# Edge-list graph layer: node marks as a one-hot in place of steps, slot-major marks turned by transposing DMAs, and a constant operand table

## The chip, the core and the metric

The kernel runs on one core of one Trainium2 chip. The metric is device microseconds of one execution of the whole program. The core has five instruction streams that matter here: TensorE (PE in the profile, with its weight loads shown apart as PEld), VectorE (DVE), ScalarE (ACT), GpSimd (POOL) and SyncE (SP), which only issues DMAs.

## The reference

128 graphs of 64 nodes with 128 features each; `adj` is a symmetric 0/1 matrix with ones on the diagonal, about one entry in eight set.

```python
f_i = jnp.broadcast_to(x[:, :, None, :], (B, P, P, C))      # B=128, P=64, C=128
f_j = jnp.broadcast_to(x[:, None, :, :], (B, P, P, C))
messages = _mlp(jnp.concatenate([f_i, f_j], -1), msg weights)   # relu, layernorm, relu, layernorm, linear
messages = messages * adj[..., None]
agg = jnp.sum(messages, axis=2)
out = x + _mlp(jnp.concatenate([x, agg], -1), upd weights)
```

Each `_mlp` is three products with a relu and a layernorm after the first two. A message counts only where `adj` is 1, so only the edges have to be computed.

## The kernel before, in words

**Edges as slots.** The kernel never forms the 64 x 64 pairs. Each graph gets 640 edge slots (`CAP`), five tiles of 128. Edge number k of a graph stands in slot k, node by node. Two graphs share the 128 partitions and form a *pair* (64 pairs, index p); two pairs form a *quad* (32 quads, index q; 20 tiles, 5 chunks); two quads form a *block* (16 blocks, index b; 10 chunks). A *chunk* is 4 tiles, 512 slots; there are 160, and the main loop has one *step* per chunk.

**What a step does.** In step n the kernel issues, in this order: `layer1(n - 8)`, the second message layer of an older chunk (lines 559 and 562, into the bank `z`, relu by ScalarE into `y`, line 565); `layer0(n)`, the first layer, as a product of node features with a 0/1 selection matrix `s` (line 513, into `hps`, relu into `h`, line 516); `stats0(n - 1)`, four transposes of `h` into the bank `hT` (line 522) and their layernorm statistics on VectorE (line 526); `marks(n + 2)` (line 498, into the bank `mk`) and `compare(n + 2)` (line 505), which make `s`; and `stats1(n - 8)`, statistics of `y` on VectorE (line 572). Then come the *extras* of the step: whatever a written table of `at(step, place, function)` has put there. The order on every engine is the order of this code; there is no scheduler that moves things. The banks `mk`, `hT`, `hps` and `z` exist once each.

**How `s` is made.** Per pair, `make_tp` (line 482, VectorE) writes a tile `tp`: partition i (a node of one of the two graphs), slot k, 1 where k is less than the running edge count of node i. It is a *step* along the slots. `marks` multiplies it with a per-block table `qs` whose columns hold differences of neighbouring nodes, so that the product becomes, per slot, the source node's one-hot in 64 rows and a position to be compared with in the other 64. The table `qs` is built per block: `place` (lines 394 to 399, GpSimd), `marks_table` (lines 384 to 387, GpSimd: copies constants and zeroes), `steps` (line 429, a product with a difference matrix `dq` on TensorE) and `steps_out` (lines 436 and 437, two ScalarE copies out of the bank `ma`).

**How messages are summed per node.** `reduce` (line 656) multiplies `y` of each tile with weights `w` (slots on the partitions, 64 nodes along the row). For `w` the marks are needed with slots on the partitions: `node_marks` (line 625) multiplies each 128 x 128 piece of `tp` with a constant matrix `pick`, five products per pair into banks `ma`; `node_marks_out` (line 632) copies them out with ScalarE into `oh`; `weights` (line 641, GpSimd; VectorE in the last quad) multiplies `oh` with the inverse standard deviations `m_q`. In a cycle of five steps the pair with even p has its `node_marks` in the step that also holds `reduce` (40 PE instructions of line 656) and `rows` (lines 457 and 459), the odd one in the step after it; `weights` follow two steps after each, `reduce` three steps after the first `weights`.

**Other extras.** `rank`, `count`, `degrees` (running counts per block), `turn_x` (line 443), `rows_hi` and `rows_lo` (lines 466, 473: the node features split in two parts `abh`, `abl`), the update MLP of an older block (lines 701, 715, 725, 751), statistics arithmetic on GpSimd (lines 254 to 272), `root1_of` (line 278, ScalarE, tile `m_sq`) and `inverse_of` (line 283, VectorE, tile `m_q`). SyncE issues the loads of `adj` (`an`) and `x` (`xn`) 20 to 25 steps ahead, and the stores of `uo` (line 754), which wait for `finish` (line 751).

Of the kernel before, what the change touches and what calls it, by code (L numbers as in the profile page):

```python
# [9 lines left out]
F32 = mybir.dt.float32  # L10
# [13 lines left out]
def tile_gnn(  # L24
# [11 lines left out]
):  # L36

# [66 lines left out]
    def load_first(b, q0, q1):  # L104
# [50 lines left out]
    nc.vector.memset(cmpt[0:N, 0:3 * CAP // 2], 1.0)  # L155
    slot = const.tile([P, CAP], F16, name="slot")
    nc.gpsimd.iota(slot, pattern=[[1, CAP]], base=0, channel_multiplier=0,
                   allow_small_or_imprecise_dtypes=True)

    dq = const.tile([P, P], F32, name="dq")  # L160
    nc.gpsimd.affine_select(out=dq, in_=ident, pattern=[[-1, P]], compare_op=ALU.not_equal,
                            fill=-1.0, base=-1, channel_multiplier=1)

    pick32 = const.tile([P, P], F32, name="pick32")
    nc.gpsimd.affine_select(out=pick32, in_=ident, pattern=[[-1, P]], compare_op=ALU.not_equal,
                            fill=-1.0, base=1, channel_multiplier=1)

    nc.gpsimd.memset(pick32[0:N, N:N + 1], 0.0)
    pick = const.tile([P, 2, N], F16, name="pick")
    nc.gpsimd.tensor_copy(pick.rearrange("p g m -> p (g m)"), pick32)  # L170
# [123 lines left out]
    def edge_path(es):  # L294
        blkp = es.enter_context(tc.tile_pool(name="blk", bufs=3))
        adp = es.enter_context(tc.tile_pool(name="adp", bufs=2))
        qsp = es.enter_context(tc.tile_pool(name="qsp", bufs=2))
# [41 lines left out]
        TP, S, H, ST0, V0, SD, SH, Y, ST1, Q, OH, WT, YS, MK = ({} for _ in range(14))  # L339
# [42 lines left out]
        def marks_table(b):  # L382
            qs = qsp.tile([P, PB, 2, P], F16, name="qs")
            nc.gpsimd.tensor_copy(qs[:, :, :, 0:N],
                                  pick.unsqueeze(1).to_broadcast([P, PB, 2, N]))
            nc.gpsimd.memset(qs[N:P, :, 0, N:P], 0.0)
            nc.gpsimd.memset(qs[0:N, :, 1, N:P], 0.0)
            blocks[b]["qs"] = qs

        def place(b):  # L390

            blk = blocks[b]
            before = adp.tile([P, PB], F32, name="before")
            nc.gpsimd.tensor_tensor(before, cumall[:, b * PB:(b + 1) * PB], blk["deg"],
                                    op=ALU.subtract)
# [3 lines left out]
            nc.gpsimd.tensor_tensor(pos, pos, blk["an"], op=ALU.mult)  # L399
            blk["pos"] = pos  # L400

# [67 lines left out]
        def rows_lo(b, half):  # L469
# [5 lines left out]
                op=ALU.subtract)  # L475
            blk["ab", half] = (lo, hi)


        def make_tp(p):

            tp = tpp.tile([P, CAP], F16, name="tp")
# [635 lines left out]
```

## Time and profile before

| | us |
|---|---|
| median of 3 runs | 645.67 (641.34 to 647.46) |
| profiled execution, whole | 640.71 |
| its span, first to last instruction | 639.0 |
| TensorE busy | 615.1 |
| VectorE busy | 497.6 |
| GpSimd busy | 368.4 |
| ScalarE busy | 358.6 |
| mean granted TensorE clock | 0.993 of full |

How to read it: the rows of the profile name an instruction by its line in the kernel, its engine, its operation and its tiles (out<-in), with the count, the busy time and the mean duration. Matmuls are pipelined: the duration of one (275 ns for most) is longer than the distance from one to the next, so for TensorE the start times of the timeline are the measure. A float32 product shows as two MATMUL rows, so counts of line 562 and its like are twice those of the code. The profiled execution lies 1.7 us above its span, and 5.0 us under the median of the runs.

### The profile page before, as it was taken

To read this page: it belongs to the slowest core of one execution; us is meant where nothing else is said; L and a number is where in the kernel's file an instruction comes from. 1 tells how busy PE (TensorE), PEld (TensorE's weight loads), DVE (VectorE), ACT (ScalarE), POOL (GpSimd) and SP (SyncE) were. 2 spreads that over 40 slices of the span, in tenths; PEclk is the share of its full clock that TensorE was granted. 3 is DMA by queue.
4 is the path that set the end of the run, shared out by engine and by line. 5 is a ranking of instruction groups with operands and counts; after the bars stand their busy time and mean duration, and the time that the engine had idled before them with its cause. 6 is when DMAs were issued, how large, how long until landed. Compare 5 with 4: busy or idle time off the path is not lost.

```text
span 639.0 us, 15850 instructions
## 1 busy us (share of the span) xinstructions
PE 615.1 (96%) x5875; PEld 567.0 (89%) x5875; DVE 497.6 (78%) x1894; ACT 358.6 (56%) x811; POOL 368.4 (58%) x943
## 2 busy tenths in 40 slices
PE   7899999999999999999999999999999999998875
PEld 6688899999999999999999999999999999997764
DVE  6787687878878787887878788787878877785574
ACT  3556556655656565565656556565655656563532
POOL 6742463847657384765738476573837657363653
PEclk8999999999999999999999999999999999999998
DMA  5100000010010101001010100101010000000001
GB/s 119 40 21 6 2 10 2 2 43 3 2 42 2 42 3 42 2 7 37 2 43 2 43 3 11 32 2 44 2 34 1 17 4 2 17 1 18 2 18 35
DMA packets 27916, 12.06 MB, mean 19 GB/s; under 512 B 10422, under 2 KB 27836, under 8 KB 27836
## 3 DMA queue, kind: packets, MB, share of 16 engines
q1 hardware_dynamic: 27548, 10.89, 6.4%
q8 instruction: 47, 0.77, 0.5%
q14 instruction: 33, 0.27, 0.1%
q10 hardware_dynamic: 288, 0.13, 0.1%
HBM read 6.82 MB, written 4.19 MB: 17 GB/s over the span
## 4 chain that ended last, share of the span: by engine, by line


## 5 line engine op out<-in xcount | busy, mean ns | idle before, releaser
L526 DVE BATCH_NORM_STATS2 st<-hT 128x6 f32<-128x128 f32 x640 | 141.1, 282 | 65.2 <-PE hT L522 62.6
L562 PEld LDWEIGHTS z<-w1c,h 128*128 128x128 f32 x1280 | 168.4, 192 | 7.1
L562 PE MATMUL z<-w1c,h 128*128 128x128 f32 x1280 | 168.8, 275 | 0.0
L641 POOL TENSOR_TENSOR w<-oh,m_q 128x320 f32<-128x320 f16 x124 | 86.9, 722 | 127.4 <-PE hT L522 110.9
L572 DVE BATCH_NORM_STATS2 st<-y 128x6 f32<-128x128 f32 x640 | 137.6, 276 | 6.0 <-ACT y L565 6.0
L565 ACT ACTIVATE y<-z 128x512 f32<-128x512 f32 x160 | 95.6, 597 | 81.4 <-PE z L562 79.5
L516 ACT ACTIVATE h<-hps,b0c 128x512 f32<-128x512 f32 x160 | 109.2, 682 | 6.1 <-PE hps L513 6.0
L505 DVE TENSOR_TENSOR s<-mk,cmpt 128x512 fp32r<-128x512 f32 x160 | 107.4, 672 | 0.4 <-PE mk L498 0.4
L522 PE MATMUL hT<-ident,h 128*128 128x128 f32 x640 | 97.0, 274 | 0.0
L513 PE MATMUL hps<-s,abl 128*128 128x512 f32 (+3 forms) x256 | 91.7, 370 | 0.0
L522 PEld LDWEIGHTS hT<-ident,h 128*128 128x128 f32 x640 | 76.2, 141 | 9.7
L559 PE MATMUL z<-b1t,sdT 80*128 80x512 f32 x160 | 78.8, 493 | 0.9 <-ACT y L565 0.9
L513 PE MATMUL hps<-s,abh 128*128 128x512 f32 (+3 forms) x256 | 78.1, 323 | 0.0
L656 PE MATMUL ys<-y,w 128*64 128x128 f32 x1280 | 76.9, 275 | 0.0
L656 PEld LDWEIGHTS ys<-y,w 128*64 128x64 f32 x1280 | 69.2, 137 | 3.4
L498 PE MATMUL mk<-tp,qs 128*128 128x512 f16 (+3 forms) x256 | 61.2, 300 | 1.8 <-DVE s L505 1.7
L473 DVE TENSOR_TENSOR abl<-mu,abh 128x512 fp32r<-128x512 f32 x32 | 22.1, 690 | 49.6 <-ACT abh L466 49.5
L632 ACT CAST oh<-ma 128x384 f16<-128x384 f32 (+1 forms) x128 | 48.6, 433 | 4.7 <-PE ma L625 1.8
L513 PEld LDWEIGHTS hps<-s,abl 128*128 128x128 f32 x256 | 49.2, 192 | 0.6 <-ACT h L516 0.3
L466 ACT CAST abh<-mu 128x512 fp32r<-128x512 f32 x32 | 18.7, 585 | 54.8 <-PE mu L459 54.8
L513 PEld LDWEIGHTS hps<-s,abh 128*128 128x128 f32 x256 | 49.1, 192 | 0.0
L559 PEld LDWEIGHTS z<-b1t,sdT 80*128 80x128 f32 x160 | 30.3, 190 | 8.9 <-issue 3.1
(235 smaller groups left out, 1036.8 us busy)
## 6 DMA issues: line engine op xcount, KB each, us to landing
xn<-in_x_dram SPq DMA_DIRECT2D x15, 256.0 KB, 3.2
out_dram<-uo SPq DMA_DIRECT2D x15, 256.0 KB, 2.2
an<-in_adj_dram SPq DMA_DIRECT2D x16, 128.0 KB, 2.9
xn<-in_x_dram SPq DMA_DIRECT2D x2, 128.0 KB
out_dram<-uo SPq DMA_DIRECT2D x2, 128.0 KB, 2.1
w<-in_L_gnn_msg_w_dram SPq DMA_DIRECT2D x2, 64.0 KB, 2.9
u<-in_L_gnn_upd_w_dram SPq DMA_DIRECT2D x2, 64.0 KB, 2.0
w0a<-in_L_gnn_msg_w_dram ACTq DMA_DIRECT2D x1, 64.0 KB, 2.1
```

The source lines that it names most:

```text
L498: nc.tensor.matmul(MK[n][:, c:c + w], lhsT=blocks[g // (2 * PB)]["qs"][:, g // 2 % PB, g % 2, :], rhs=TP[g // 2][:, e:e + w], start=True, ...
L505: nc.vector.tensor_tensor(S[n], MK.pop(n), cmpt[:, o:o + CH * P], op=ALU.is_equal)
L513: nc.tensor.matmul(ps[:, c:c + w], lhsT=ab[:, g % 4, :], rhs=s[:, c:c + w], start=(k == 0), stop=(k == 1))
L516: nc.scalar.activation(H[n], ps, AF.Relu, bias=b0c)
L522: nc.tensor.transpose(ps[:, t, :], H[n][:, t * P:(t + 1) * P], ident)
L526: nc.vector.bn_stats(ST0[q][:, CH * c + t, :], ps[:, t, :])
L559: nc.tensor.matmul(ps, lhsT=SD[q], rhs=W["b1t"][:, CH * c:CH * c + CH, :], start=True, stop=False, skip_group_check=True)
L562: nc.tensor.matmul(ps[:, t, :], lhsT=h[:, t * P:(t + 1) * P], rhs=W["w1c"], start=False, stop=True, skip_group_check=True)
L565: nc.scalar.activation(Y[n], ps, AF.Relu)
L572: nc.vector.bn_stats(ST1[q][:, CH * c + t, :], Y[n][:, t, :])
L641: (nc.vector if p // 2 == NQ - 1 else nc.gpsimd).tensor_tensor(w[:, :, g, :], OH[p][:, :, g, :], Q[q][:, k:k + TG].unsqueeze(2).to_broadca ...
L656: nc.tensor.matmul(YS[b][g * N:(g + 1) * N, k, :], lhsT=w[:, t, g, :], rhs=y, start=(t == 0), stop=(t == TG - 1))
```

## The change

Three things are changed together.

1. `tp` becomes a one-hot: 1 in the slots that belong to node i. ScalarE first writes a distance `d` = |mid - (2k + 1)| (`distance`, new), where `mid` is the sum of the running counts before and after the node; VectorE then compares `d` with the node's degree (`make_tp`, same shape as before). With a one-hot, the table needs no differences: `steps` (TensorE), `steps_out` (ScalarE) and `dq` go.
2. The slot-major marks `oh` are the transpose of the one-hot, so `node_marks` becomes one transposing DMA per pair, issued by SyncE, SBUF to SBUF, 128 x 640 float16. It is issued four steps earlier than the products were (two in the last quad), so six steps ahead of `weights`, whose place stays. `pick`, the five products and `node_marks_out` go. `oh` gets four buffers.
3. The table is now `qsall`, two constant halves used by blocks in turn: the identity part and the zeros are written once at the start, and `place_out` (GpSimd, two instructions on 64 partitions) writes only the positions. `marks_table` goes. `place_out` and `odd_marks` stand one step later than `place`.

```diff
+    qsall = const.tile([P, 2, PB, 2, P], F16, name="qsall")
+    for k in range(2):
+        nc.vector.memset(qsall[:, k], 0.0)
+        nc.gpsimd.tensor_copy(qsall[:, k, :, :, 0:N], ident.rearrange("p (g m) -> p g m", g=2)
+                              .unsqueeze(1).to_broadcast([P, PB, 2, N]))
...
-        def marks_table(b):
-            qs = qsp.tile([P, PB, 2, P], F16, name="qs")
-            nc.gpsimd.tensor_copy(qs[:, :, :, 0:N],
-                                  pick.unsqueeze(1).to_broadcast([P, PB, 2, N]))
-            nc.gpsimd.memset(qs[N:P, :, 0, N:P], 0.0)
-            nc.gpsimd.memset(qs[0:N, :, 1, N:P], 0.0)
...
+            blk["mid"] = adp.tile([P, PB], F32, name="mid")
+            nc.gpsimd.tensor_tensor(blk["mid"], cum, before, op=ALU.add)
...
-            nc.gpsimd.tensor_tensor(pos, pos, blk["an"], op=ALU.mult)
+        def place_out(b):
+            for g in range(2):
+                s = slice(g * N, (g + 1) * N)
+                nc.gpsimd.tensor_tensor(qsall[s, b % 2, :, g, N:P], pos[s], blk["an"][s],
+                                        op=ALU.mult)
...
-        def steps(b):
-            nc.tensor.matmul(blk["ps"][:, 0:PB * N], lhsT=dq,
-                             rhs=blk.pop("pos").rearrange("p q j -> p (q j)"), start=True,
-                             stop=True)
-        def steps_out(b):
-            nc.scalar.copy(blk["qs"][0:N, :, 0, N:P], psv[0:N])
-            nc.scalar.copy(blk["qs"][N:P, :, 1, N:P], psv[N:P])
...
+        def distance(p):
+            D[p] = tpp.tile([P, CAP], F16, name="d", bufs=3)
+            nc.scalar.activation(D[p], slot, AF.Abs, bias=blocks[b]["mid"][:, q:q + 1], scale=-1.0)
         def make_tp(p):
-            nc.vector.tensor_scalar(tp, slot, cumall[:, p:p + 1], None, op0=ALU.is_lt)
+            nc.vector.tensor_scalar(tp, D.pop(p), blocks[b]["deg"][:, q:q + 1], None,
+                                    op0=ALU.is_lt)
...
         def node_marks(p):
-            for t in range(TG):
-                nc.tensor.matmul(ps[:, k * P:(k + 1) * P], lhsT=TP[p][:, t * P:(t + 1) * P],
-                                 rhs=pick.rearrange("p g m -> p (g m)"), start=True, stop=True)
-        def node_marks_out(p):
-            for ps, t, n in zip(OH[p], (0, 3), (3, TG - 3)):
-                nc.scalar.copy(o[:, t:t + n].rearrange("p t g m -> p (t g m)"), ps[:, 0:n * P])
+            OH[p] = wp.tile([P, TG, P], F16, name="oh", bufs=4)
+            nc.sync.dma_start(OH[p], TP.pop(p), transpose=True)
...
-                at(o - 8, "e", marks_table, b)
-                at(o - 8, "e", odd_marks, b)
+                at(o - 7, "e", place_out, b)
+                at(o - 7, "e", odd_marks, b)
-                at(o - 4, "x", steps, b)
-                at(o - 3, "a", steps_out, b)
...
+                at(n - 5 if n >= 5 else 0, "a", distance, p)
                 at(n - 4, "m", make_tp, p)
-            at(m, "x", node_marks, p)
-            at(m + 1, "a", node_marks_out, p)
+            at(w - 4, "a", node_marks, p)
```

Where the rows stand, at the three places that matter. TensorE, in the step after `reduce` (the odd pair of a quad); before, `tp` is the weight operand of five products with `pick`, between the marks and the next step's `z`:

```order
L522 MATMUL hT<-ident,h 128x128 x4
L498 LDWEIGHTS qs
L498 MATMUL mk<-tp,qs 128x128
L498 LDWEIGHTS qs
L498 MATMUL mk<-tp,qs 128x384
L625 LDWEIGHTS tp
L625 MATMUL ma<-pick,tp 128x128
```

and, after four more such pairs of rows, line 559 of the next step. Of the change, the same place (line numbers are those of the changed file, 5 to 19 lower):

```order
L517 MATMUL hT<-ident,h 128x128 x4
L493 LDWEIGHTS qsall
L493 MATMUL mk<-tp,qsall 128x128
L493 LDWEIGHTS qsall
L493 MATMUL mk<-tp,qsall 128x384
L554 MATMUL z<-b1t,sdT 128x512
L557 MATMUL z<-w1c,h 128x128 x4
```

The five products are gone and the next step's `z` follows the marks at once: the step holds nothing beside its regular work.

SyncE, one block of the steady state. Before, it issues one store and two loads:

```order
L754 DMA out_dram<-uo 128x4x128
L355 DMA xn<-in_x_dram 128x4x128
L347 DMA an<-in_adj_dram 128x4x64
L754 DMA out_dram<-uo 128x4x128
L355 DMA xn<-in_x_dram 128x4x128
```

Of the change, with four transposes between the same DMAs:

```order
L736 DMA out_dram<-uo 128x4x128
L615 DMA_TRANSPOSE oh<-tp 128x5x128
L350 DMA xn<-in_x_dram 128x4x128
L615 DMA_TRANSPOSE oh<-tp 128x5x128 x2
L342 DMA an<-in_adj_dram 128x4x64
L615 DMA_TRANSPOSE oh<-tp 128x5x128
L736 DMA out_dram<-uo 128x4x128
```

Each transpose now stands behind a store or a load on one queue, and one of the four stands right behind the store that waits for `finish`.

GpSimd, from the step of `place` to the next `weights`. Before (`m_v`, `m_d`, `m_s`: statistics of a quad, which end in `m_sq` and `m_q`; `a`: `odd_marks`):

```order
L397 TENSOR_TENSOR pos<-rk,before 128x256
L399 TENSOR_TENSOR pos<-pos,an 128x256
L384 COPY qs<-pick 128x8x64
L386 MEMSET qs 64x4x64
L387 MEMSET qs 64x4x64
L417 TENSOR_TENSOR a_3252<-an 128x256
L418 TENSOR_TENSOR a_3252<-a_3252,an 128x256
L270 TENSOR_SCALAR m_v<-m_2801 128x20
L254 TENSOR_TENSOR m_d<-st_2975 128x20
```

Of the change:

```order
L384 TENSOR_TENSOR mid<-cumall,before 128x4
L386 TENSOR_TENSOR pos<-rk,before 128x256
L266 TENSOR_SCALAR m_v<-m_2699 128x20
L250 TENSOR_TENSOR m_d<-st_2871 128x20
L251 TENSOR_TENSOR m_s<-st_2871 128x20
L252 TENSOR_TENSOR m_d<-m_d 128x20
L253 TENSOR_SCALAR m_d<-m_d 128x20
L254 TENSOR_TENSOR m_3201<-m_d,m_s 128x20
L268 TENSOR_TENSOR m_v<-m_v,m_3201 128x20
L395 TENSOR_TENSOR qsall<-pos,an 64x4x64 x2
L418 TENSOR_TENSOR a_3210<-an 128x256
```

The statistics now come before the table and `odd_marks`, not behind them.

More of the change, by code (lines that the diff above doesn't have):

```diff
@@ L859, in edge_path @@
         turn_x_out(0, 0, 2)
+        degrees(0)
         place_first()
[L861 to L862 removed]
+        distance(0)
+        place_pair(0)
+        make_tp(0)
         rows(0, 0)
         rows_hi(0, 0)
[L866 to L874 removed]
+        distance(1)
+        place_pair(1)
+        make_tp(1)
         marks(0)
```

71 lines of the change are left out of this document (21 added, 50 removed).

## Prediction, on record before the result

> **What bounds the kernel now.** I read the page's busy times first, then its 40 slices, then stretches of the span, then TensorE's own starts.
>
> ```profile
> PE 615.1 (96%) x5875; PEld 567.0 (89%) x5875; DVE 497.6 (78%) x1894; ACT 358.6 (56%) x811; POOL 368.4 (58%) x943
> PE   7899999999999999999999999999999999998875
> 200.00:270.00 70.00, 70.00 (x695) 65.74 (x695) 57.67 (x223) 40.63 (x91) 41.16 (x106) 1.00 0.08 20
> 580.00:600.00 20.00, 16.14 (x156) 14.66 (x156) 12.28 (x57) 7.95 (x19) 8.90 (x20) 1.00 0.05 14
> ```
>
> A stretch reads: length, busy PE, PEld, DVE, ACT, POOL, granted clock, DMA share, GB/s. In 200 to 270 us TensorE is busy for all 70 us at full clock, VectorE for 58. The slices say the same from about 45 to 580 us. Only the start and the last 60 us have gaps. The page's chain that ended last is empty, so the waits have to say what stops TensorE; its two longest are small, with three and four cases in the whole run:
>
> ```profile
> PE ma L701 <- DVE uy L247: 4.2, 3, 2.6
> PE ma L546 <- POOL sh L541: 4.0, 4, 1.5
> ```
>
> So work taken off TensorE between 45 and 580 us shortens the program by what it occupies there, as long as nothing else comes late. What it occupies is not its busy time, since matmuls overlap. It is read from starts (start, duration, operation, count):
>
> ```profile
> 301.35 0.58 PE L559 MATMUL z<-b1t,sdT 80*128 80x512 f32 x1
> ...
> 317.44 0.60 PE L429 MATMUL ma<-pos,dq 128*128 128x256 f32 x2
> 317.88 0.27 PE L546 MATMUL ma<-ident,sh 128*80 128x128 f32 x1
> ...
> 328.04 1.05 PE L562 MATMUL z<-w1c,h 128*128 128x128 f32 x8
> 330.05 0.44 PE L625 MATMUL ma<-pick,tp 128*128 128x128 f16 x5
> 330.30 0.48 PE L559 MATMUL z<-b1t,sdT 80*128 80x512 f32 x1
> 330.62 1.05 PE L562 MATMUL z<-w1c,h 128*128 128x128 f32 x8
> ...
> 336.72 1.05 PE L562 MATMUL z<-w1c,h 128*128 128x128 f32 x8
> ...
> 338.55 0.58 PE L559 MATMUL z<-b1t,sdT 80*128 80x512 f32 x1
> 338.97 1.05 PE L562 MATMUL z<-w1c,h 128*128 128x128 f32 x8
> ...
> 341.06 0.44 PE L625 MATMUL ma<-pick,tp 128*128 128x128 f16 x5
> 341.43 2.40 PE L656 MATMUL ys<-y,w 128*64 128x128 f32 x40
> ```
>
> From one step's line 562 to the next is 2.25 us in a step without extras (336.72 to 338.97) and 2.58 in the step whose only extra is line 625 (328.04 to 330.62). The odd pair's five products cost 0.33 us. The even pair's stand in front of line 656 and cost 341.43 - 341.06 = 0.37. Line 429 costs 317.88 - 317.44 = 0.44 per block.
>
> **TensorE's part of the sum.** A quad loses 0.33 + 0.37 = 0.70 us. Of 32 quads I count 29: the last six groups of line 625 lie after 583 us, where TensorE has gaps and waits decide. 29 x 0.70 = 20.3. Line 429 runs for blocks 1 to 15: 15 x 0.44 = 6.6. Together **26.9 us**. The most it could be, with every pair and the even price, is 64 x 0.37 + 6.6 = 30.3.
>
> **The other engines, by rows.**
>
> ```profile
> L632 ACT CAST oh<-ma 128x384 f16<-128x384 f32 (+1 forms) x128 | 48.6, 433 | 4.7 <-PE ma L625 1.8
> L437 ACT CAST qs<-ma 64x256 f16<-64x256 f32 x15 | 5.5, 367 | 0.2
> L449 ACT COPY xnT<-ma 128x512 f32<-128x512 f32 (+1 forms) x16 | 9.1, 572 | 16.6 <-PE ma L443 16.6
> L482 DVE TENSOR_SCALAR tp<-slot,cumall 128x640 f16<-128x640 f16 x64 | 24.4, 383 | 0.0
> L399 POOL TENSOR_TENSOR pos<-pos,an 128x256 f32<-128x256 f32 x15 | 11.2, 744 | 1.2
> L384 POOL COPY qs<-pick 128x512 f16<-128x512 f16 x16 | 9.8, 614 | 0.1
> L387 POOL MEMSET qs<- 64x256 f16 x16 | 4.9, 308 | 0.9
> L394 POOL TENSOR_TENSOR before<-cumall,deg 128x4 f32<-128x4 f32 x15 | 3.0, 201 | 3.9 <-ACT deg L380 3.9
> ```
>
> ScalarE loses 48.6 us of line 632 and two rows like line 437 (11.0), and gains 64 distances of 640 columns. No row shows one. From the copy of 512 columns, 572 x 640 / 512 = 0.72 us, 46 in all; not under 0.57 (fewer columns), and at the rate of line 632, which carries 320 columns in 0.433, 0.87, 55 in all. ScalarE ends 4 to 23 us lighter. The copies of the even pair leave a step and a distance enters the bare one; with ScalarE busy 40.6 of 70 us in the stretch above, 0.72 more in one step finds room. VectorE's `tp` keeps shape and type: 0.38 each, no change. GpSimd loses 0.74 + 0.61 + 2 x 0.31 = 1.97 per block and gains `mid` (0.20) and two products of 256 columns (0.74 each if length decides, as in line 399; 0.31 if it goes like the zeroing): 0.8 to 1.7. I take the upper one; it is still 0.3 lighter.
>
> **Does a shorter step wait for VectorE?** VectorE's regular work per step follows from these rows, and so does its slack:
>
> ```profile
> 308.18 0.69 DVE L473 TENSOR_TENSOR abl<-mu,abh 128x512 fp32r<-128x512 f32 x1 [1.45 <-ACT abh L466]
> 309.78 0.89 DVE L526 BATCH_NORM_STATS2 st<-hT 128x6 f32<-128x128 f32 x4 [0.91 <-PE hT L522]
> 310.59 0.67 DVE L505 TENSOR_TENSOR s<-mk,cmpt 128x512 fp32r<-128x512 f32 x1
> 311.18 0.86 DVE L572 BATCH_NORM_STATS2 st<-y 128x6 f32<-128x128 f32 x4
> ...
> 339.94 0.67 DVE L505 TENSOR_TENSOR s<-mk,cmpt 128x512 fp32r<-128x512 f32 x1
> 340.84 0.38 PE L498 MATMUL mk<-tp,qs 128*128 128x512 f16 x1
> ```
>
> Statistics 0.81, compare 0.59, statistics 0.8: about 2.2 us against 2.25 of a bare step. Now three steps in ten are bare instead of one. The old bare step is the tight one: there the compare of 339.94 ends 0.23 us before the next marks want its bank. Nothing is removed from that step or the one ahead of it, so its slack stays. The two new bare steps are those of the odd pair, and there VectorE waits today 1.45 and then 0.91 us for others; losing 0.33 leaves it idle time. No cost.
>
> GpSimd's chain into `m_sq` gets shorter where it was late:
>
> ```profile
> 306.64 0.73 POOL L399 TENSOR_TENSOR pos<-pos,an 128x256 f32<-128x256 f32 x1
> 310.11 0.27 POOL L270 TENSOR_SCALAR m_v<-m 128x20 f32<-128x20 f32 x1
> 311.96 0.31 ACT L278 ACTIVATE m_sq<-m_v,eps_c 128x20 f32<-128x20 f32 x1 [1.04 <-POOL m_v L272]
> ```
>
> Lines 399 to 418 (306.64 to 310.1) now come behind the statistics, so `m_v` starts some 3 us sooner, while TensorE arrives 0.7 us sooner. What comes later is `odd_marks` and the table, needed five steps on.
>
> **The transposes.** No transposing DMA is in the trace, so its price is bounded by the plain ones:
>
> ```profile
> q1 hardware_dynamic: 27548, 10.89, 6.4%
> xn<-in_x_dram SPq DMA_DIRECT2D x15, 256.0 KB, 3.2
> SPq L754 <- DVE uo L751: 500.0, 16, 51.6
> ```
>
> A load of 256 KB lands in 3.2 us. The queue's 27,548 packets took 6.4% of 16 engines over 639 us, 654 us, 23.7 ns each. A transpose moves 128 x 640 x 2 = 163,840 bytes. In pieces of 256 bytes that is 640 packets, 640 x 23.7 / 16 = 0.95 us; of 32 bytes 7.6 us; of 2 bytes (element by element) 121 us. A block of ten steps takes 37.2 us now (line 559 from 301.35 to 338.55) and 2 x 0.70 + 0.44 less after, 35.4, for four transposes: one may take **8.8 us** before the queue itself sets the pace. For latency there are six steps, 21 us. SyncE stands at the store for most of the time (500 us waiting for `uo`), so one transpose in four can't be issued before `finish`; that is the step ahead of its place, and six steps remain. I take 3 to 8 us, near the 256 KB row, **hidden** by those six steps of TensorE work; if that cover were gone, each microsecond beyond costs one per quad.
>
> The Trainium skill, "VectorE: DVE Perf Modes", section "The three transpose paths", gives 1309 ns for a 128 x 128 16-bit transpose by DMA against 390 ns on TensorE, and advises TensorE where a PSUM destination will do. That speaks against this change by the single operation. Five in a row would be 6.5 us per pair by it, an estimate, under the bound above; and the trace shows why the single price misleads: TensorE's 0.33 to 0.37 us are on the engine that sets the end.
>
> **The start** is a chain of single waits: `adj` lands, `rank` at 3.5 us, the first compare at 9.0.
>
> ```profile
> 3.50 0.69 DVE L362 TENSOR_TENSOR_SCAN rk<-first,an 128x256 f32<-128x256 f32 x1 [1.14 <-DMA an<-in_adj_dram]
> 7.95 0.43 DVE L872 CAST qs<-z 64x256 f16<-64x256 f32 x1 [0.51 <-PE z L868]
> ```
>
> It loses the two `dq` products of line 868 and the copy that waits for them (to 8.38), and gains `mid` and two distances that VectorE must wait for, one of them queued behind `abh` on ScalarE. I work it out at 0.5 us later, between 1 us earlier and 1.5 later.
>
> **Sum.** 26.9 - 0.5 = 26.4 us. The profiled execution is 640.7, which gives **614.3**. The three runs have their median 5.0 us above it and their lowest 0.6 above; taking about a third of that distance, I say **616 us**.
>
> **Rivals.**
> - *The transposes set the pace (slower).* If the pieces are 16 bytes, a transpose is 15.2 us, a block 61, and 16 blocks with start and end about 1020 us; it decides at 8.8 us each, pieces of 28 bytes. For it: no row shows such a DMA, and the elements that it turns are only 2 bytes wide. Against: 32 bytes already suffice. Chance 0.12. The page's 6.5 us would stay below that point.
> - *The gain is taken back by waits.* Where new bare steps wait for VectorE or `oh`, the odd pairs' 29 x 0.33 = 9.6 and half the rest are lost, 26.4 down to about 8.5: 632. For it: VectorE's 2.2 us in a 2.25 us step. Against: its idle 0.9 and 1.45 us there. Chance 0.11.
> - *Nothing comes of it.* The landing comes about 0.8 us per quad too late (a latency of 22 us), the wait replaces the products: 641. Against: 3.2 us for a bigger load. Chance 0.05.
>
> **How the numbers follow.** Forecast 0.72, between 605 (30.3 from TensorE, the start 1 us better, some waits gone at the end) and 624. With the half-lost case the range is 605 to 634, which leaves out the no-change and the slow case. A change under 1% can't be told from none here. Faster 0.83, same 0.05, slower 0.12.
>
> **What would show it.** Right: lines 625, 632, 429 are gone, PE busy falls by about as much as the span, a step after `reduce` shrinks to 2.25 us, VectorE's share rises to about 81%, and `weights` waits for `m_q`, not for a DMA. Wrong: TensorE idle at `ys` with GpSimd behind `oh` (transposes), or idle at `hT` or `mk` behind VectorE (second rival), or transposes landing in over 9 us.

## The result, and the profile after

The changed kernel takes **626.16 us** (median of 4 runs, 624.33 to 626.91) against 644.62 (641.34 to 647.46) for the kernel before on the same chip: a ratio of **0.971, 95% interval 0.966 to 0.976**, 18.5 us. Forecast were 616 us, 605 to 634. The direction and the outer range hold. The narrower range of the forecast itself, 605 to 624, was missed by 2 us, and the gain is 0.70 of the 26.4 us that the sum promised.

The profiled execution takes 626.91 us with a span of 625.1. Between the two profiled executions the gain is smaller, 13.8 us: the one before (640.7) was faster than all four of its runs, the one after is the slowest of its four. First the page's busy times, then the same stretches as before:

```profile
PE 595.2 (95%) x5521; PEld 545.6 (87%) x5521; DVE 497.8 (80%) x1900; ACT 348.2 (56%) x716; POOL 363.3 (58%) x922
...
200.00:270.00 70.00, 69.81 (x672) 64.87 (x671) 58.17 (x225) 41.44 (x84) 42.89 (x112) 1.00 0.19 39
580.00:600.00 20.00, 16.24 (x156) 14.85 (x157) 12.62 (x50) 7.22 (x16) 14.99 (x34) 1.00 0.12 31
600.00:625.00 25.00, 14.23 (x124) 11.67 (x120) 12.96 (x48) 5.06 (x15) 7.88 (x25) 0.80 0.08 24
```

TensorE's busy time fell by 19.9 us, the span by only 13.9. In 200 to 270 us TensorE is no longer quite full: 0.19 us of 70 are idle. The waits name the place (PE is the matmul, PEld its weight load, which shows the wait better; total, times, longest). The first two rows are of the changed kernel, the third of the kernel before, whose PE row stands in the prediction:

```profile
PE ma L541 <- POOL sh L536: 5.6, 6, 2.0
PEld ma L541 <- POOL sh L536: 10.5, 18, 2.3
PEld ma L546 <- POOL sh L541: 5.3, 5, 1.9
```

The wait for the split root `sh`, four cases (PE) and five (PEld) before, now comes about once in each block. What a block is made of is read from starts of layer 1's products (line 557, before 562). Of the change, TensorE's timeline:

```profile
320.79 1.05 PE L557 MATMUL z<-w1c,h 128*128 128x128 f32 x8
323.04 1.05 PE L557 MATMUL z<-w1c,h 128*128 128x128 f32 x8
325.72 1.05 PE L557 MATMUL z<-w1c,h 128*128 128x128 f32 x8
329.06 0.31 PE L541 MATMUL ma<-ident,sh 128*80 128x128 f32 x1
329.43 1.05 PE L557 MATMUL z<-w1c,h 128*128 128x128 f32 x8
331.68 1.05 PE L557 MATMUL z<-w1c,h 128*128 128x128 f32 x8
333.56 0.38 PE L493 MATMUL mk<-tp,qsall 128*128 128x512 f16 x1
333.87 2.40 PE L638 MATMUL ys<-y,w 128*64 128x128 f32 x40
337.42 1.06 PE L557 MATMUL z<-w1c,h 128*128 128x128 f32 x8
339.66 1.05 PE L557 MATMUL z<-w1c,h 128*128 128x128 f32 x8
```

337.42 to 339.66 is the step of the odd pair, 2.24 us where it was 2.58. 331.68 to 337.42 is that of the even pair, 5.74. 325.72 to 329.43, 3.71, is a step with a root's turn (line 541) at its end, and it has grown. The same step before is 3.42, from 333.30 to 336.72:

```profile
333.30 1.06 PE L562 MATMUL z<-w1c,h 128*128 128x128 f32 x8
336.37 0.27 PE L546 MATMUL ma<-ident,sh 128*80 128x128 f32 x1
336.72 1.05 PE L562 MATMUL z<-w1c,h 128*128 128x128 f32 x8
```

The same over all blocks (medians of twelve, in us, each step from line 557 to line 557):

| step | before | after | products back | root later |
|---|---|---|---|---|
| even pair, two per block | 6.01 | 5.73 | 6.00 | 5.74 |
| odd pair, two per block | 2.58 | 2.24 | 2.57 | 2.24 |
| root, behind the update's eight products | 3.42 | 3.71 | 3.41 | 3.31 |
| the step that had line 429 | 4.74 | 4.31 | 4.31 | 4.20 |
| the other four | 11.86 | 11.85 | 11.86 | 12.06 |
| block of ten steps | 37.20 | 35.83 | 36.75 | 35.55 |

The two right columns belong to experiments below. The block saves 1.37 us, where the sum had 2 x 0.70 + 0.44 = 1.84.

The transposes, from the page's DMA issues and queues, and from the view of the tile `oh` (issue in ns, min/median/max):

```profile
oh<-tp SPq DMA_TRANSPOSE x64, 2.5
...
q1 hardware_dynamic: 70556, 21.38, 15.8%
```
```profile
L615 SPq DMA_TRANSPOSE oh<-tp x64: 1198/1202/2408, 13.9 to 582.4; - x64
```

They land 2.5 us after their issue (2.4 to 4.3), and none of the engines' longer waits is for one of them.

### The profile page after: what moved, and what is told of

It is laid out like the page before. It is cut to its first block, busy times and chain, and to the rows that moved or that the text cites. A ratio compares the mean times of both kernels' runs of the same rounds, so it can differ in the third digit from the quotient of the medians.

```text
span 625.1 us, 15119 instructions
## 1 busy us (share of the span) xinstructions
PE 595.2 (95%) x5521; PEld 545.6 (87%) x5521; DVE 497.8 (80%) x1900; ACT 348.2 (56%) x716; POOL 363.3 (58%) x922
## 5 line engine op out<-in xcount | busy, mean ns | idle before, releaser
L554 PE MATMUL z<-b1t,sdT 80*128 80x512 f32 x160 | 80.5, 503 | 1.4 <-ACT y L560 1.4
L493 PE MATMUL mk<-tp,qsall 128*128 128x512 f16 (+3 forms) x256 | 61.8, 303 | 3.5 <-DVE s L500 2.4
L470 ACT ACTIVATE d<-slot,mid 128x640 f16<-128x640 f16 x64 | 52.6, 823 | 0.7 <-DVE mid L404 0.7
```

The costliest lines, as they stand in the source:

```text
L493: nc.tensor.matmul(MK[n][:, c:c + w], lhsT=qsall[:, g // (2 * PB) % 2, g // 2 % PB, g % 2, :], rhs=TP[g // 2][:, e:e + w], start=True, sto ...
L554: nc.tensor.matmul(ps, lhsT=SD[q], rhs=W["b1t"][:, CH * c:CH * c + CH, :], start=True, stop=False, skip_group_check=True)
```

## The experiments

All times are medians; each ratio is against runs of the kernel before on the same chip. The experiments ran on three chips, so those of different chips are compared by their ratios and by their profiles.

| kernel | us (lowest to highest, runs) | ratio, 95% |
|---|---|---|
| changed kernel again | 626.92 (623.66 to 627.22, 6) | 0.970 (0.968 to 0.973) |
| variance first | 628.87 (626.47 to 630.58, 6) | 0.974 (0.971 to 0.977) |
| root turned later | 621.82 (619.43 to 623.12, 6) | 0.963 (0.961 to 0.966) |
| start reordered | 624.74 (623.78 to 626.94, 6) | 0.968 (0.966 to 0.971) |
| products back | 641.37 (640.57 to 644.11, 10) | 0.996 (0.993 to 0.998) |
| transposes late | 626.38 (626.10 to 627.39, 4) | 0.972 (0.968 to 0.976) |
| transposes left out | 625.70 (625.59 to 628.05, 4) | 0.971 (0.966 to 0.975) |
| end filled | 625.76 (625.62 to 626.41, 6) | 0.971 (0.968 to 0.974) |
| weights behind the split | 625.53 (622.42 to 626.76, 6) | 0.968 (0.965 to 0.971) |
| before, root turned later | 641.36 (639.89 to 645.70, 6) | 0.992 (0.989 to 0.995) |
| best version | 614.61 (614.35 to 614.72, 5) | 0.952 (0.950 to 0.955) |
| best, unfilled | 615.24 (615.15 to 615.39, 5) | 0.954 (0.952 to 0.956) |

### The changed kernel again

> The changed kernel once more, on the chip on which the next three run, so that they can be set against it. Every theory: about 0.971 of the kernel before (0.966 to 0.976), a block of ten steps in 35.8 us, and the step in which the root of a quad is turned in 3.70 us. If the tail's and the start's half-speed stretches are chance, they lie elsewhere in this profile; if they follow from waits of TensorE, they lie at the same places.

626.92 us, and its profile repeats that of the first to 0.2 us, by chunk and at the end, its stretches at half clock at the same places. So the differences below are read against the changed kernel's profile as well.

### Where the gain is: the products put back

```diff
-            OH[p] = wp.tile([P, TG, P], F16, name="oh", bufs=4)
-            nc.sync.dma_start(OH[p], TP.pop(p), transpose=True)
...
+            for t in range(TG):
...
+                nc.tensor.matmul(ps[:, k * P:(k + 1) * P], lhsT=TP[p][:, t * P:(t + 1) * P],
+                                 rhs=ident16, start=True, stop=True)
...
```

The products go into a PSUM bank, and ScalarE copies them out one step later.

> Everything of the change is kept (one-hot, distance, constant table, no step product) but the transposing DMAs: each pair's marks are turned again by five TensorE products with a 16-bit identity, at the steps of the kernel before, and copied out by ScalarE. Theory (the gain is TensorE time of the turning products, and little else): the step with the odd pair's products goes from 2.24 to 2.58 us and the one with the even pair's from 5.73 to 6.0 us, a block of ten steps from 35.83 to 37.0 us less what the root wait gives back (0.3 us), 36.8 us; the whole is 15 to 16 us above the changed kernel, 642 us, or 0.994 of the kernel before. Rival (half of the gain or more is that ScalarE and VectorE are relieved): no more than 8 us above the changed kernel, 634 us or less.

641.37 us and a block of 36.75, where the theory had 36.8. Five products cost 0.33 us in the odd step and 0.27 in the even one, and putting them back takes the root's wait away again:

```profile
PEld ma L543 <- POOL sh L538: 5.9, 5, 2.3
```

Its 2 x 0.33 + 2 x 0.27 - 0.29 is 0.91 against 0.92 measured. The step that held line 429 stays at 4.31: of the whole gain about 15 us are the turning products, and the rest is the step product, less what the start loses. ScalarE carries both the distances and the copies here (388.8 us busy), and no step is longer for it than the kernel before had it.

### Are the transposes hidden?

```diff
-            at(w - 4, "a", node_marks, p)
+            at(w - 1 if last else w + 1, "a", node_marks, p)
```

> Each transposing DMA is issued five steps later, one step ahead of the weights that read it. Theory (it lands 2.5 us after its issue, and a step is 3.6 us): hidden still, 626 us within 1.5 us, block 35.83 us; at the most GpSimd's weights wait a few tenths of a us for it, off the path. Rival (the lead of six steps is what hides it, the queue being slow under load): GpSimd waits for the marks at the weights line, the root's chain behind them on GpSimd comes late by as much, and the time is 632 us or more.

```diff
-            OH[p] = wp.tile([P, TG, P], F16, name="oh", bufs=4)
-            nc.sync.dma_start(OH[p], TP.pop(p), transpose=True)
+            if p < 2:
+                nc.sync.dma_start(oh_c[p], TP[p], transpose=True)
+            del TP[p]
+            OH[p] = oh_c[p % 2]
```

> The transposing DMAs are left out but for the first two, whose result stands for all the other pairs (so the sums per node are of other data). Theory (64 transposes cost nothing beside the engines' work): 626 us within 1.5 us, block 35.83 us, the same durations of VectorE and GpSimd operations. Rival (their reads and writes of SBUF or their queue slow the engines or the loads): 2 us or more below the changed kernel, with shorter durations of some group of instructions.

626.38 and 625.70 us; the block is 35.83 and 35.82. One step of lead is enough, and without them nothing is faster. Leaving out 62 transposes takes 41,664 packets off the queue:

```profile
q1 hardware_dynamic: 28892, 11.22, 6.8%
```

That is 672 packets for each. By their sizes in the trace, 640 of them hold 256 bytes and 32 hold 4. All take 9% of the 16 engines' span, which is 0.9 us of the 16 engines for one. The operations beside them keep their lengths (the weights on GpSimd 721 ns without, 723 with them). Hidden, and by a wide margin.

### What took a part back: the root of a quad

The root's chain goes VectorE statistics, five GpSimd operations (`m_d` to `m`), ScalarE's root and cast, GpSimd's split (`sh`), TensorE's turn. On GpSimd in the changed kernel:

```profile
325.36 1.40 POOL L623 TENSOR_TENSOR w<-oh,m_q 128x320 f32<-128x320 f16 x2 [6.69 <-PE mk L493]
326.72 0.25 POOL L250 TENSOR_TENSOR m_d<-st 128x20 f32<-128x20 f32 x1
...
327.83 0.23 POOL L254 TENSOR_TENSOR m<-m_d,m_s 128x20 f32<-128x20 f32 x1
328.73 0.27 POOL L536 TENSOR_TENSOR sh<-m_sd,sh 128x40 fp32r<-128x40 f32 x1 [0.68 <-ACT sh L535]
328.96 1.41 POOL L623 TENSOR_TENSOR w<-oh,m_q 128x320 f32<-128x320 f16 x2
```

Everything here starts with the weights (line 623) at 325.36, and they start when VectorE has made `m_q`. The row puts their wait down to `mk`; but in 29 of 31 quads they start 0.13 us behind the end of `m_q`, and in the kernel without the transposes, where it is 0.14 or 0.15 us in all but one, the profile names `m_q` for the whole wait:

```profile
L626 POOL TENSOR_TENSOR w<-oh,m_q 128x320 f32<-128x320 f16 x124 | 86.8, 721 | 116.5 <-DVE m_q L280 116.5
```

VectorE, from the step of the odd pair on, first in the changed kernel, then with the products put back:

```profile
322.79 0.89 DVE L521 BATCH_NORM_STATS2 st<-hT 128x6 f32<-128x128 f32 x4 [0.91 <-PE hT L517]
...
324.97 0.26 DVE L279 RECIPROCAL m_q<-m_sq 128x20 f32<-128x20 f32 x1
```
```profile
329.66 0.89 DVE L523 BATCH_NORM_STATS2 st<-hT 128x6 f32<-128x128 f32 x4 [0.90 <-PE hT L519]
...
331.84 0.26 DVE L281 RECIPROCAL m_q<-m_sq 128x20 f32<-128x20 f32 x1
```

Between the two rows VectorE takes 2.18 us in both, without a pause; its 0.9 us of idle time lie ahead of the first. In those 2.18 us TensorE ends the odd pair's step, with or without the five products. So `m_q` stands 0.75 us ahead of the next step's layer 1 in the one (325.72) and 1.08 in the other (332.92, below), as in the kernel before (1.09): 0.33 us later as TensorE counts, and weights, variance and split all with it.

```profile
332.92 0.72 PE L559 MATMUL z<-w1c,h 128*128 128x128 f32 x5
```

Before I had seen that, I took the weights ahead of the variance for the whole delay, and queued the variance ahead of them:

```diff
+        for q in range(NQ):
+            at(q * QC + QC, "e1", var0_of, q)
         for p in range(NP):
...
         for q in range(NQ):
...
-            at(n, "e1", var0_of, q)
```

> The five GpSimd operations of a quad's layer-0 variance are queued ahead of the weights of the step and not behind them. Theory (TensorE's new wait for the split root comes from the weights, 2 x 0.72 us, which stand ahead of the variance on GpSimd while TensorE now arrives 0.34 us earlier): the wait of 10.5 + 5.6 us for the root falls below 4 us, the step that turns the root goes from 3.70 back to 3.4 us, a block from 35.83 to 35.55 us, and the whole 15 blocks gain about 4 us: 622 us. Rival (the chain ends on ScalarE's root and cast, which have their own queue): no change, 626 us within 1.5.

It got slower: 628.87 us, the step 3.82 and the block 35.94. So the theory, which had forecast 622, is wrong as I had put it, and so is the rival of no change. The same rows of this kernel say why:

```profile
326.47 0.25 POOL L250 TENSOR_TENSOR m_d<-st 128x20 f32<-128x20 f32 x1 [7.38 <-DVE st L521]
...
327.53 0.23 POOL L254 TENSOR_TENSOR m<-m_d,m_s 128x20 f32<-128x20 f32 x1
327.71 1.60 POOL L623 TENSOR_TENSOR w<-oh,m_q 128x320 f32<-128x320 f16 x2
329.27 0.27 POOL L536 TENSOR_TENSOR sh<-m_sd,sh 128x40 fp32r<-128x40 f32 x1
```

The chain visits GpSimd twice. The weights had been ahead of the first visit; now they sit between the two, 327.71 to 329.3, while ScalarE is done with the cast at 328.35 (it starts at 328.13 and takes 0.22). `m_d`, too, could not start before the statistics. The mended order keeps the variance first and puts the even pair's weights behind the split:

```diff
-            at(NCHK + L1 + 1 if last else w + 2, "e1", weights, p)
+            at(NCHK + L1 + 1 if last else w + 3 - p % 2, "e1", weights, p)
```

> As the variance-first kernel, and the even pair's weights are queued one step later on GpSimd, behind the split of the root and not between the variance and the split. Theory, as mended by that kernel's trace (the chain of the root passes GpSimd twice, and whatever stands between its two passes delays it as much as what stands ahead): both passes are free of the weights, TensorE's wait for the root falls below 3 us in sum, the step that turns the root goes from 3.71 to about 3.35 us and the time to 621.5 us, as where TensorE's order was changed. Rival one (the chain is bound by VectorE's statistics and ScalarE): 3.6 us or more for that step and 625 us or more. Rival two (the weights are now late for the sums per node): a wait of GpSimd's weights at the sums' line and 628 us or more.

```profile
325.78 0.23 POOL L254 TENSOR_TENSOR m<-m_d,m_s 128x20 f32<-128x20 f32 x1
326.69 0.27 POOL L536 TENSOR_TENSOR sh<-m_sd,sh 128x40 fp32r<-128x40 f32 x1 [0.68 <-ACT sh L535]
326.92 2.76 POOL L623 TENSOR_TENSOR w<-oh,m_q 128x320 f32<-128x320 f16 x4
```

The split now comes 0.9 us behind the variance, the step is 3.41 and the block 35.53: in the blocks the mended theory holds. The time doesn't show it: 625.53 against 621.5 forecast, which is where the first rival had it. By chunk, the profiled execution loses 1.5 us against the changed kernel before chunk 5, wins 4.9 up to chunk 155 and loses 2.4 behind it. The loss at the start is the clock's (below): it lies in the step of chunk 0, 5.01 us where it was 3.56, and the end-filled kernel, which has the order of the changed one, takes 4.88 there; both ran at half clock for 6.8 us from 28.8 and 28.6 us on, the changed kernel for 3.4. Of the loss at the end 1.3 us are the order's. Near 578 us all four weights now stand between the split and GpSimd's statistics of the update (`um_v`), where only two stood; ScalarE waits for those statistics with its `y` queued behind, and TensorE waits 2.08 us for `y` where it waited 0.7:

```profile
585.59 0.30 ACT L274 ACTIVATE um_sq<-um_v,eps_c 128x4 f32<-128x4 f32 x1 [3.79 <-POOL um_v L268]
586.91 0.50 PE L554 MATMUL z<-b1t,sdT 80*128 80x512 f32 x1 [2.08 <-ACT y L560]
```

The remaining 1.1 us go with a stretch at half clock of 6.8 us near the end, where the changed kernel has one of 3.4.

TensorE's own order was the other way in:

```diff
-            at(n + 1, "x", turn_root, q)
-            at(n + 2, "a", root_out, q)
+            at(n + 2, "b", turn_root, q)
+            at(n + 2, "b", root_out, q)
```

> The order on TensorE alone is changed: the turn of a quad's root and its copy out stand behind the next step's layer 1 and not at the end of their own step; GpSimd's order stays. Theory (only the wait for the root is new, nothing behind it): the wait is covered by the layer 1 of one chunk (about 1 us), so the result is that of the variance queued first, 3.7 to 3.4 us in that step and 4 us in all: 622 us. Rival one (the layer 1 that uses the root now comes so soon behind the copy that TensorE waits there instead): 626 to 632 us, with a wait for the turned root at the layer-1 line in its place. Rival two (the step is bound elsewhere): 626 us.

621.82 us as forecast, the root's step 3.31, the block 35.55. (0.11 us of the 0.40 is the turn itself, which now counts in the next step.) The wait is left at two places, the first and the last quad:

```profile
PE ma L541 <- POOL sh L536: 2.0, 2, 1.7
```

The profiled execution is 3.6 us ahead by the blocks (from 3.13 at chunk 20 to 6.75 at chunk 140) and 3.1 by the start, where it has no stretch at half clock at 28 us (below); that alone is worth 1.6. That the wait came with the change, and was not worth mending before, is what the next one asks:

> The kernel before, with the root of a quad turned behind the next step's layer 1, as was done to the changed kernel. Theory (the wait for the root came with the change, since TensorE arrives earlier): here it is worth next to nothing in the steady blocks, 37.2 us to 37.1 or 37.2 us, and the time is within 1.5 us of the kernel before (0.998 to 1.002). Rival (the wait was there all along): 4 to 5 us faster, 0.993.

The blocks answer as the theory forecast: 37.20 us before, 37.19 with the root later. The time doesn't: 4.5 us less, 0.992, which is the rival's number. The profiled execution wins 1.8 us in the first 20 chunks, loses 2.6 between chunk 155 and the last layer 1 and is, with a span of 641.5 against 639.0, not faster. Its six runs lie from 639.9 to 645.7; four of them were granted a mean clock of 0.990, where nine of the eleven of the kernel before had 0.986 to 0.988. So the saving isn't in the blocks, and where it is in the other runs stays open. It also means that the 5.1 us of the same edit in the changed kernel do not show by themselves what the wait costs: that is read from the blocks, 3.6 us from chunk 20 to 140.

### The start and the end

```diff
-        distance(1)
-        place_pair(1)
-        make_tp(1)
         marks(0)
         rows_lo(0, 0)
         compare(0)
+        distance(1)
+        place_pair(1)
+        make_tp(1)
```

The second half of the table moves to step 0 on GpSimd in the same kernel.

> Distance, placed marks and one-hot of pair 1 stand behind the first comparison and not ahead of it, and the second half of the constant operand table (a fill and a cast) is made in step 0 on GpSimd and not ahead of the first scan. Theory (the start lost time because work that is needed only from chunk 2 on stood ahead of chunk 0 on VectorE): the first comparison starts 1.5 to 2 us earlier (9.86 to about 8.1 us after the span's start), and the end comes 1.5 to 2 us earlier: 624.3 us. Rival (the first root's chain on GpSimd, which ends at 27.6 us, takes it back): the first comparison is earlier all the same, but TensorE's wait for the root at 25.6 us grows by as much and the end moves by less than 0.5 us.

624.74 us, 2.2 less, though the runs of the two overlap. In the profile layer 1 of chunk 0 starts 1.4 us earlier than in the changed kernel, but that one ran at half clock for 3.4 us behind the turn of its first root, and this one did not. The variance-first and the late-transposes kernel, which are like it in that, have their first compare at 10.38 us and layer 1 of chunk 0 at 32.16 and 32.23 us; here it is 9.28 and 31.07, so the reordering is worth 1.1 us. The clock column reads 1.00 for the first 20 us of all three, and that is misleading: their traces record no clock before 16.1, 17.2 and 17.3 us, and up to there the same four products take nearly twice as long as behind:

```profile
13.47 1.05 PE L519 MATMUL hT<-ident,h 128*128 128x128 f32 x4
16.35 0.60 PE L519 MATMUL hT<-ident,h 128*128 128x128 f32 x4
```

VectorE's compare starts at 9.28, not at 8.1: it now waits for ScalarE, which has `distance(0)` ahead of the cast `abh`.

```profile
8.68 0.69 DVE L463 TENSOR_TENSOR abl<-mu,abh 128x512 fp32r<-128x512 f32 x1 [0.79 <-ACT abh L456]
9.28 0.68 DVE L502 TENSOR_TENSOR s<-mk,cmpt 128x512 fp32r<-128x512 f32 x1
```

The wait for the first root, 1.97 us, is neither better nor worse, so the rival's taking back did not happen either.

```diff
+        def fill(k):
...
+        at(167, "x2", fill, 8)
+        at(169, "x2", fill, 16)
```

> 24 products of no use are added to TensorE's order near the end, 8 and 16, in the two waits (1.4 and 2.7 us) behind the last chunk, where the kernel before had the last pairs' turning products for a part. Theory (the end is 2 us longer than before, 30.8 against 28.7 us from the last layer 1, since TensorE idles there and its clock is halved in the stretch that follows): the halved stretch is gone, the end takes about 29.0 us and the time is 1.5 to 2 us less, 624.7 us. Rival (the half-speed stretch comes at a fixed place or by chance): the end stays at 30.7 us or grows by up to 0.5 us, and the time is 626.5 us.

From the last layer 1 to the end it is 29.9 us, where the changed kernel has 30.8 and the kernel before 28.7: half of the forecast, and 625.76 us is within the spread. The filling took part of its gain back: TensorE is still at the added products when `uy` is there, and turns it 11.8 us behind the last layer 1, where the changed kernel did so at 10.9.

More telling is the end over all profiles: 30.1 us in the kernel before with its root later, and 30.3 with the products put back. Both have all their products, and both have, as the changed kernel, a stretch of 3.4 us at half clock at the wait of 2.6 us for `uy`. So 1.4 to 1.6 of the 2.1 us come without the change; the remaining 0.5 to 0.7 is not explained. The profiled execution of the kernel before, at 640.7 us one of its fastest, has the same wait and no such stretch behind it. Its last 25 us:

```profile
614.00:639.00 25.00, 14.55 (x144) 0.88 0.12 34
```

The granted clock (the column behind TensorE's busy time) is 0.88, where the changed kernel's row above, its last 25 us, has 0.80. The Trainium skill, "TensorE: Matmul & The Clock Gate", Part 1, puts the gate on free-running windows of 3.4 us, so that the same kernel comes out differently from run to run. The traces agree: in every profile that has several stretches at half clock they start at whole multiples of 3.41 us from each other, and the same start ran at half clock for 3.4 us in the end-filled kernel (from 11.5 us on), for 6.8 in the changed one (from 7.6), and until 17.3 us in the late-transposes kernel. What one such stretch costs can be read at the wait of 2.27 us for the flag's bank, near 565 us in the changed kernel. Ten of the twelve profiles that have this wait run at half clock behind it. The other two are the kernel before and the end-filled kernel, whose order is the changed kernel's there; it takes 35.5 us from chunk 145 to 155, the changed kernel 37.1. That is 1.6 us for the clock alone.

### The best version

> The changed kernel with the root turned later (but for the last quad), the pair-1 work and the second half table behind the first comparison, the first quad's variance on VectorE and the constant bias table's parts 1 to 4 made two steps later (both shorten the first root's chain on GpSimd), the sum of the flag in a bank of its own at the end, and the filling products. Theory (the parts add, each at its own place): 5 us of the root's wait, 1.1 of the start, about 1 of the first root, 1 to 2 of the flag's wait and 1 of the end, 9 to 10 us: 616.5 us, 0.957 of the kernel before. Rival (what is won at the start and the end is taken back by the next wait there): 620.5 us or more, 0.963.

```diff
-            V0[q] = square_sum(stp, ST0.pop(q), QT, "m20", eng_of(q))
+            V0[q] = square_sum(stp, ST0.pop(q), QT, "m20",
+                               nc.vector if q == 0 else eng_of(q))
...
-            at(n + 1, "x", turn_root, q)
-            at(n + 2, "a", root_out, q)
+            at(n + 1 if q == NQ - 1 else n + 2, "x" if q == NQ - 1 else "b", turn_root, q)
+            at(n + 2, "a" if q == NQ - 1 else "b", root_out, q)
...
-            at(4 + c, "e", bias_part, c)
+            at(6 + c if c else 4, "e", bias_part, c)
...
-            FL["b"] = ubank()
+            FL["b"] = abank()
```

This comes with the start reordered and the end filled as above. **614.61 us, 0.952 of the kernel before**, 12.3 us under the changed kernel and more than the 10 forecast. By chunk, against the changed kernel: 2.6 us by the first layer 1, 4.4 more up to chunk 140 (of which 3.6 are blocks), 3.9 between chunks 145 and 155, where TensorE had waited 2.27 us for the flag's bank and lost 1.6 at half clock behind that, and 0.9 at the end. TensorE's windows around that wait, first the changed kernel, then this one, which comes there some 10 us sooner:

```profile
560.00:580.00 20.00, 17.73 (x151) 0.91 0.13 31
```
```profile
552.00:572.00 20.00, 18.33 (x168) 1.00 0.27 39
```

> The best version without its 24 filling products at the end. Theory (the idle 1.4 and 2.7 us of TensorE behind the last chunk bring on a half-speed stretch, which is also what scatters the times over 3 us): a stretch at half clock after the 2.7 us wait, 1 to 2 us more, 615.6 to 616.6 us, and a spread of the runs over 1 us where the best version's was 0.4 us. Rival (the filling was worth nothing once the rest was mended): 614.6 us within 0.5, spread as small.

615.24 us, 0.6 more on another chip; the intervals of the two ratios overlap. In the profiles the end is 0.4 us longer without the filling (30.4 against 29.9). The stretch at half clock behind the 2.7 us wait is there again, 3.4 us from 595.3 on, and yet the spread of the runs is as small as with the filling (0.24 us). So the theory that the idle end scatters the times is wrong. Both versions scatter by less than 0.4 us where all others do by 0.8 to 6; which of the edits does that was not tried apart.

## Why the prediction was right, and where it was not

- **The bound.** Right: TensorE set the pace between 45 and 580 us, and the products taken off it show in the block nearly one for one, as their return shows.
- **What was luck.** The forecast itself, 616 in 605 to 624, was too low: 626.2 lies outside it, and inside 605 to 634 only because the range took in the case of the second rival. Of the signs named, TensorE's busy time did not fall by about as much as the span (19.9 against 13.9 us); lines 625, 632 and 429 are gone, the step after `reduce` is 2.24 us, VectorE's share is 80%, and no wait of `weights` is for a DMA.
- **The odd pair and line 429.** 0.33 and 0.44 forecast, 0.34 and 0.43 measured in a step. The first had been read as the difference of a whole step, the second from start to start, and there it held. But two of the fifteen products of line 429, at 24.6 and 58.1 us, saved nothing: one stands ahead of the first layer 1, and the step of the other takes 4.14 us before and after. That is 0.9 us.
- **The even pair, mis-sized.** 0.37 forecast, 0.28 measured (0.27 when put back). It was read from start to start, 341.06 to 341.43. That interval holds a part which stays: from the marks (line 493) to `ys` it was 340.84 to 341.43, 0.59, and is now 333.56 to 333.87, 0.31. The difference is the price, 0.28. Over the 29 quads the term was 2.7 us too big.
- **"... losing 0.33 leaves it idle time. No cost.": the step that failed.** VectorE's idle time in the odd pair's step is there, 0.91 us before and after, but it lies ahead of the statistics that TensorE must first turn for it, so it buffers nothing. What follows runs at VectorE's own pace, 2.18 us to `m_q`, then the weights, the variance and the split, a chain of fixed length that had just been on time. Against a TensorE that is 0.34 us sooner it is late at `sh`, whose row stood in the prediction and was passed over as small. The second rival was of this kind, but looked for the wait at VectorE and `oh` themselves. It costs 0.29 us in nearly every block, 0.62 in one, 4.6 us in all. Two experiments, the split freed on GpSimd and TensorE's turn moved, bring the block to 35.53 and 35.55.
- **The transposes.** Hidden, as forecast. The landing is 2.5 us, below the 3 to 8 I took, below the 6.5 us estimated for five single transposes in a row, and next to the plain loads; SyncE's order behind the store cost nothing. The pieces are of 256 bytes, 640 for each, and take 0.9 us of the 16 engines, where the prediction had 0.95 for this case. So the rival that they set the pace, with its pieces of 16 bytes, is refuted.
- **ScalarE, VectorE, GpSimd.** The distance takes 0.82 us, inside 0.57 to 0.87 and above the 0.72 taken; the two GpSimd products 0.73 each, the upper end. Neither is on the path. `m_sq` waits 0.6 us for `m_v` in the whole run where it waited 12.5. TensorE waits for VectorE itself in neither of the new bare steps.

```profile
L470 ACT ACTIVATE d<-slot,mid 128x640 f16<-128x640 f16 x64 | 52.6, 823 | 0.7 <-DVE mid L404 0.7
...
L395 POOL TENSOR_TENSOR qsall<-pos,an 64x256 f16<-64x256 f32 x30 | 21.8, 728 | 1.2
L274 ACT ACTIVATE m_sq<-m_v,eps_c 128x20 f32<-128x20 f32 x32 | 9.8, 308 | 0.6 <-POOL m_v L268 0.6
```

- **The start.** Forecast 0.5 us later, at most 1.5. Layer 1 of chunk 0 is 2.5 later in the profiled execution, but the first compare only 0.8 (9.86 against 9.02), and from there to the turn of the first root both take 17.76 us. The other 1.6 us lie behind that turn, where the changed kernel runs at half clock from 28.1 us on: from it to the first layer 1 takes 4.86 us, 3.22 in the kernel before, and 3.23 in the three kernels with the changed order on TensorE that run at full clock there. So the forecast was near. What it had not seen is pair 1's work and the second half table, as operations of VectorE ahead of the first compare: 1.1 us by the reordered start.
- **The base.** The sum stood on an execution near the fast end of the kernel before. Where the profiled execution of the change has stretches of 3.4 us at half clock behind the first root, the flag's wait and the wait for `uy`, that of the kernel before has none: 1.6, 1.6 and 1.4 to 1.6 us, which are no effect of the change. In the experiments' runs of the kernel before, those with a mean clock of 0.993 took 640.7 to 643.0 us and those with 0.986 to 0.990 643.5 to 647.3.

From 614.3 to 626.9 for the profiled executions, step by step: 2.7 (even pair) + 0.2 (odd pair) + 0.9 (line 429) + 4.6 (root) + 2.0 (start, 1.6 of it the clock's) + 1.3 (the two steps at the flag's wait, 1.6 less the 0.3 that one of them saved) + 2.1 (end, 1.4 to 1.6 of it the clock's) = 13.8 us. Against that stand 1.2 us that the last three quads saved, which the sum had left out. Together this is 12.6 of 12.6 us.

## What to carry to other kernels

When work is taken off the engine that sets the pace, list every chain on other engines that today arrives just in time, however small its wait: its consumer moves earlier, and the chain only as far as what starts it does; idle time counts as slack only where it lies behind the operation that waits, not ahead of it. If such a chain visits an in-order engine twice, look at what is queued between the visits before reordering ahead of the first; it is often simpler to move the consumer. Price a removed group by whole steps with and without it, and compare several executions, with their clocks, before a difference of 2 us at the start or the end is called an effect.

## What the runs showed of the hardware

- A transpose by DMA of 128 x 640 16-bit elements from SBUF to SBUF landed in 2.5 us, as 640 packets of 256 bytes and 32 of 4, beside loads and stores, without a measurable effect on any engine (a block takes 35.83 us with them and 35.82 without); SyncE spent 1.2 us on issuing one.
- TensorE's clock was halved for 3.4 us, in places twice as long, behind the wait of 2.27 us in ten of twelve profiles and behind that of 2.6 us in eleven of twelve, and behind the first root's wait of 1.98 us in some kernels and not in others. One such stretch cost 1.6 us at the first wait, 1.4 to 1.6 at the second and 1.6 at the third. A pair of profiles compared without it would have put almost 5 us on the change.
- The clock column of a profile read 1.00 over the first 16 to 17 us of three traces in which TensorE ran at half speed there (1.05 us for four products, 0.60 behind): nothing was recorded before the first change of clock. The durations of like products tell the clock where the column can't.
